# Layer 0 of a four-layer convolution stack: how the first expansion of a block, the first image's loads and the last block's residual rows are arranged

## The chip, the cores and the metric

The kernel runs on one core of one Trainium2 chip, as one launch. The metric is the device time in microseconds (us), the median of several runs. The engines are called by their short names: PE (TensorE, matmuls; PEld is its loading of stationary operands), DVE (VectorE), ACT (ScalarE), POOL (GpSimd) and SP (SyncE, which here only issues DMAs).

## The reference, cut to what matters

Input x is (4, 64, 256, 256) in float32. Four layers follow one another, each `x = x + f(groupnorm(x))`. The change touches layer 0 alone:

```python
def _L0_conv_ref(x, w_in, w_dw, fft_filter, w_out):
    p = PATCH                                             # 8
    x = jnp.einsum('bchw,oc->bohw', x, w_in)              # 64 -> 384 channels
    B, C, H, W = x.shape
    xp = x.reshape(B, C, H // p, p, W // p, p).transpose(0, 1, 2, 4, 3, 5)
    xp = jnp.fft.irfft2(jnp.fft.rfft2(xp) * fft_filter, s=(p, p))
    x = xp.transpose(0, 1, 2, 4, 3, 5).reshape(B, C, H, W)
    x = lax.conv_general_dilated(x, w_dw, window_strides=(1, 1), padding=[(1, 1), (1, 1)], feature_group_count=C)
    x1, x2 = jnp.split(x, 2, axis=1)
    x = jax.nn.gelu(x1, approximate=False) * x2
    return jnp.einsum('bchw,oc->bohw', x, w_out)          # 192 -> 64 channels
...
x = x + _L0_conv_ref(_gn(x), L0_conv_w_in, L0_conv_w_dw, L0_conv_fft_filter, L0_conv_w_out)
```

The group norm takes the mean and variance of pairs of channels over a whole image, so all of an image must have been read before any of it can be normalized.

## The kernel before, in words

**Blocks.** Layer 0 cuts each of the four images into three blocks of 11 rows of 8x8 patches (`NR = 11`), twelve blocks in all, p = 0 to 11. A block is worked through four times, kb = 0 to 3, each time for a quarter of the hidden channels. I call such a pass a quarter.

**A quarter** has two stages. The *expansion* (`expand`, L459) makes the 64-to-384 matmul with the normalized patches as the stationary operand and writes the result, patch by patch, into one SBUF tile `u`. It goes in steps (`steps_of`, L450): 11 or 12 a quarter, for eleven or twelve rows of patches. A step has two forms. With `pairs`, one stationary holds two neighbouring patches (64 x 128, L470): 16 matmuls, which the profile lists as 32 records, and four copies of 64 x 384 on ACT and four on DVE to bring the result from PSUM to `u` (L486). Without, each patch is a stationary of its own (64 x 64, L476): 32 matmuls, 64 records, and three copies on each engine (L488 to L490). The condition is on L789: the steps t = 0 to 5 of every quarter are in the first form, the rest in the second. PSUM has four tiles of two banks, and a step takes two of them, one for ACT and one for DVE.

The *convolution* joins the patchwise filter and the 3 x 3 convolution into one, by weights `wt` that are computed at the start. Per group g of four channels, `own` (L514) multiplies each patch by its own weights (L523) and `beside` (L528) adds what comes from the neighbours (L539). ACT then takes the Gelu (L546), DVE multiplies (L547), and POOL stores the tile `h` to a DRAM tile `g` (L550). The loop on L802 takes two groups at a time, g = 0, 2, ..., 10.

**The projection lags by one block.** While block p is expanded and convolved, `project` (L605) makes the 192-to-64 matmul (L627, L634) of block p - 1 in 16 units: row class r = 0 to 7 of the patch, two halves each. A unit needs two tiles read back from `g` (`load_g`, L569), and the residual rows r of the input (`load_r`, L591, rows of 128 floats, 512 bytes). DVE adds (L643 to L648), and after a second half it takes the statistics for the next layer (L654) and POOL stores the rows (L658). Each unit, when done, issues the loads of the unit two later (`unit`, L742). A block's first two units have their loads issued by the list `first`. In the first quarter the residual rows of r = 0 are ordered after step 0, the first half of `g` after the last step (L792), the second half at g = 0 (L807), and the four units stand at g = 4, 6, 8, 10. In the other three quarters the four units stand at g = 0, 2, 6, 8 (L805).

**What sets the order.** PE, DVE, ACT and SP carry out their instructions in the order in which the Python emits them; a semaphore wait holds up what is behind it on the same engine only. SP issues loads in program order and isn't held by PE's place in the program, only by free buffers and by data. POOL's order is made by the framework's scheduler.

**The start (L677 to L710).** Image 0 is read in 32 parts of 8 rows (`first_stats`, L683), and DVE takes statistics of each (`input_stats`, L313). The first ten parts read are those of block 0; they are kept in SBUF, in four tiles of the pool `p_x` and six of `p_f`, since block 0 is normalized from them. The other 22 go through three tiles of the pool `p_s`. Ahead of part 0, 10 and 20, DVE builds a table (`tables`, L334), and ACT and POOL copy it into weight tiles that POOL stores to DRAM (`weights`, L375). Then the group norm of image 0 follows (L710), whose power is taken on POOL (L217), and block 0's normalizing starts.

**The end (p = NB, L732).** After the last convolution the 16 units of the last block are left alone. The tile `u` is given up, six `g` tiles of each kind and three residual tiles take its place, and loads run three row classes ahead, on SP and ACT. Layer 1 begins by the group norm of the last image.

Of the kernel before, what the change touches and what calls it, by code (L numbers as in the profile page):

```python
# [118 lines left out]
class _Net:  # L119
# [152 lines left out]
    def _layer0(self, ctx, dst):  # L272
# [10 lines left out]
        P = PATCH  # L283
# [307 lines left out]
        def load_r(p, r):  # L591
            lo, hi, j0, rr = rows_in(p, r)
            rt = rts[p, r] = sources[p == NB - 1][2].tile([128, NR, HW2], F32, tag="r", name=f"r_{p}_{r}")[:, 0 : hi - lo]
            for s in range(2):
                nc.sync.dma_start(
                    rt[halves[s]], xr(a["x"][blocks[p][0]])[rr][:, j0 : j0 + hi - lo, s * HW2 : (s + 1) * HW2]
                )
# [79 lines left out]
        with ordered:  # L677
# [4 lines left out]

            def first_stats(k):  # L683
                if k >= NJ:
                    return
                if k < len(kept):
                    load_x(kept[k], p_x if k < 4 else p_f)
                    parts[k] = x0[kept[k]]
                    return
                t = parts[k] = p_s.tile([128, 4, W], F32, tag="x", name=f"st_{k}")  # L690
                for s in range(2):
                    nc.sync.dma_start(t[halves[s]], src_t[0, :, k, s])
# [5 lines left out]
            for k in range(len(kept) + 3):  # L698
                first_stats(k)
            copies = [nc.scalar.copy, nc.gpsimd.tensor_copy, nc.scalar.copy]  # L700
            for k in range(NJ):
                if k % 10 == 0 and k < 30:
                    tables(k // 10)
                    weights(k // 10, copies)
                input_stats(parts.pop(k), k, bst0)
                if k >= len(kept):
                    first_stats(k + 3)
# [21 lines left out]
            for p in range(NB + 1):  # L729
# [49 lines left out]
                for kb in range(4):  # L779
                    for t in range(NR + 1):  # L780
# [7 lines left out]
                        if t < len(steps):  # L788
                            expand(p, kb, steps[t], t < (NR + 1) // 2)  # L789
                        if t == 0 and kb == 0 and 0 < p:  # L790
                            load_r(p - 1, 0)
                        if t == NR:  # L792
                            if first:
                                load_half(*first.pop(0))
# [7 lines left out]
                    for g in range(0, NG, 2):  # L802
                        if g > 0:
                            load_w(p * (HID // 8) + (NG * kb + g) // 2 + 3)
                        if g in ((0, 2, 6, 8) if kb else (4, 6, 8, 10)):  # L805
                            unit()
                        if g == 0 and first:  # L807
                            load_half(*first.pop(0))
# [11 lines left out]
                        if kb == 3:  # L820
                            normalize_rows(2)
                            continue
# [734 lines left out]
```

## Time and profile before

| | us |
|---|---|
| median of 3 runs | 6439.4 |
| lowest, highest run | 6436.1, 6456.2 |
| the profiled execution, its own time | 6447.1 |
| its span, first to last instruction | 6445.2 |
| mean granted PE clock | 0.954 of full |
| norm of image 0 ready (L218, DVE) | 124.7 |
| first matmul of block 0, of block 1, of block 11 (L470) | 127.5, 395.1, 3453.2 |
| end of the last convolution of layer 0 (L539) | 3750.2 |
| end of the last projection matmul of layer 0 (L634) | 3875.9 |
| first convolution matmul of layer 1 (L940) | 3891.8 |

All times inside the execution count from the span's first instruction. In the profile's groups, a row gives line, engine, operation, output and input with the shape, then the busy time in us, the mean duration of one in ns, and the idle time ahead of them with what ended most of it. "issue" there is time in which an engine waited for nothing that the profile shows. In the table of windows, each row is a stretch, with the busy time of PE, PEld, DVE, ACT and POOL (number of instructions in brackets), the granted PE clock, the mean busy share of the 16 DMA engines and what they moved in GB/s. In the timeline, a row gives start, duration, engine, line, operation and number of instructions merged, and in square brackets the idle time ahead with what ended it.

### The profile page before, as it was taken

Reading aid. Unit: us, or ns where it says so; the run is one execution under the profiler, and the core shown is the slowest. Engines: PE = TensorE matmul, PEld = TensorE weight load, DVE = VectorE, ACT = ScalarE, POOL = GpSimd, SP = SyncE. Lnnn points to the kernel's source line nnn. Section 1 sums busy time; section 2 is a strip of 40 time slices with the busy share of each in tenths; the row PEclk is TensorE's granted clock in tenths of the full one; section 3 lists DMA queues with packets and bytes.
Section 4 is the critical chain, followed back from the end, with each engine's and each line's share of the span. In section 5 each row is a group of like instructions: output and inputs, shape, how many; then the busy total and the mean of one; then the engine's idle time right before and its main releaser. Section 6 shows DMA issues by size and latency. Waiting matters only on the chain.

```text
span 6445.2 us, 237146 instructions
## 1 busy us (share of the span) xinstructions
PE 5961.0 (92%) x106198; PEld 3303.0 (51%) x106198; DVE 4282.4 (66%) x5939; ACT 3245.7 (50%) x4575; POOL 1059.0 (16%) x1651
## 2 busy tenths in 40 slices
PE   1999999999999999999999969999899999998997
PEld 1556555555555655555565533333344444443566
DVE  5556565666566666655565638999788988885265
ACT  3444444444343535343445406777787877773211
POOL 4111111111111111111111111111122222221011
PEclk9999999999999999999999969999999999999855
DMA  7477878887888877777878699999566666678899
GB/s 198 150 216 227 224 221 231 245 228 234 224 243 235 233 217 226 224 229 223 230 217 223 191 228 239 226 230 227 145 172 172 174 173 180 173 185 278 307 362 395
DMA packets 769610, 1442.23 MB, mean 224 GB/s; under 512 B 77412, under 2 KB 463476, under 8 KB 766548
## 3 DMA queue, kind: packets, MB, share of 16 engines
q1 hardware_dynamic: 616388, 917.72, 53.7%
q0 software_dynamic: 148672, 500.14, 23.2%
q8 instruction: 839, 13.75, 0.9%
q10 hardware_dynamic: 3536, 9.20, 0.6%
q14 instruction: 175, 1.43, 0.1%
HBM read 926.71 MB, written 500.04 MB: 221 GB/s over the span
## 4 chain that ended last, share of the span: by engine, by line
PE 76%; issue 7%; DVE 7%; DMA 6%; ACT 3%; POOL 1%; SPq 0%; POOLq 0%; DVEq 0%; ACTq 0%
PE pc L539 17%; PE pc L523 11%; PE m L940 10%; PE one L1181 9%; PE div L1140 7%; PE psu L470 4%; DVE u L486 4%; PE psu L476 4%; PE po L627 4%; PE psz L1170 2%; PE po L634 2%; DMA x<-x 2%; PE psa L1368 2%; ACT u L486 1%; DMA g<-g 1%
## 5 line engine op out<-in xcount | busy, mean ns | idle before, releaser
L547 DVE TENSOR_TENSOR h<-h,pc 128x374 f32<-128x374 f32 x1152 | 576.9, 542 | 1203.4 <-ACT h L546 1203.2
L546 ACT ACTIVATE h<-pc 128x374 f32<-128x374 f32 x1152 | 495.2, 480 | 1728.7 <-PE pc L539 1727.6
L539 PE MATMUL pc<-u,w 64*16 64x374 f32 (+2 forms) x27648 | 1186.2, 479 | 12.5 <-issue 12.5
L550 POOL DMA_DIRECT2D g<-h x576 | 417.9, 726 | 2888.4 <-DVE h L547 2810.5
L523 PE MATMUL pc<-u,w 64*64 64x374 f32 x9216 | 835.8, 485 | 28.3 <-DVE u L490 21.1
L539 PEld LDWEIGHTS pc<-u,w 64*16 64x16 f32 (+2 forms) x27648 | 465.7, 92 | 698.5 <-issue 664.1
L486 DVE COPY u<-psu 64x384 f32<-64x384 f32 x1152 | 640.1, 556 | 50.6 <-PE psu L470 31.3
L470 PE MATMUL psu<-win,xn 64*128 64x96 f32 x9216 | 618.3, 277 | 36.1 <-ACT u L486 24.9
L486 ACT COPY u<-psu 64x384 f32<-64x384 f32 x1152 | 592.3, 514 | 109.8 <-PE psu L470 78.7
L470 PEld LDWEIGHTS psu<-win,xn 64*128 64x128 f32 x9216 | 582.0, 188 | 93.3 <-ACT u L486 33.6
L1126 DVE TENSOR_TENSOR q<-xn 128x2313 f32<-128x2313 f32 (+2 forms) x256 | 627.6, 2494 | 1.7 <-ACT xn L253 1.7
L1181 PE MATMUL one<-z,wp 32*32 32x512 f32 x16384 | 595.0, 597 | 21.1 <-issue 17.1
L253 ACT ACTIVATE xn<-x,nb,r 128x1024 f32<-128x1024 f32 (+3 forms) x267 | 475.3, 1802 | 204.0 <-DMA x<-x 143.1
L523 PEld LDWEIGHTS pc<-u,w 64*64 64x64 f32 x9216 | 365.9, 133 | 397.6 <-issue 158.3
L476 PE MATMUL psu<-win,xn 64*64 64x96 f32 x16384 | 468.5, 253 | 89.0 <-issue 55.3
L1127 ACT ACTIVATE q<-q 128x2313 f32<-128x2313 f32 (+2 forms) x256 | 529.0, 2087 | 31.3 <-DVE q L1126 30.2
L1181 PEld LDWEIGHTS one<-z,wp 32*32 32x32 f32 x16384 | 369.6, 103 | 227.5 <-issue 84.4
L476 PEld LDWEIGHTS psu<-win,xn 64*64 64x64 f32 x16384 | 407.3, 138 | 145.7 <-issue 83.2
L1140 PE MATMUL div<-q,ones 64*32 64x512 f32 x8192 | 469.9, 598 | 11.0 <-ACT q L1127 9.2
L1214 POOL DMA_DIRECT2D x<-r x512 | 275.7, 545 | 976.3 <-DVE r L1211 961.8
L627 PE MATMUL po<-g,wo 128*64 128x176 f32 (+1 forms) x3072 | 316.3, 348 | 64.8 <-DMA g<-g 37.9
L940 PE MATMUL m<-t,wk 64*64 64x512 f32 x3072 | 341.1, 588 | 0.0
(157 smaller groups left out, 6636.9 us busy)
## 6 DMA issues: line engine op xcount, KB each, us to landing
g<-h POOLq DMA_DIRECT2D x576, 374.0 KB, 6.9
x<-x SPq DMA_DIRECT2D x240, 640.0 KB, 6.4
w<-wt SPq DMA_DIRECT2D x288, 448.0 KB, 6.8
x<-x SPq DMA_DIRECT2D x100, 1024.0 KB, 14.1
g<-g SPq DMA_DIRECT2D x414, 187.0 KB, 7.5
g<-g SPq DMA_DIRECT2D x736, 93.5 KB, 6.9
x<-in_x_dram SPq DMA_DIRECT2D x256, 256.0 KB, 8.0
x<-o POOLq DMA_DIRECT2D x128, 512.0 KB, 8.2
```

Source lines behind the costliest of these rows:

```text
L470: nc.tensor.matmul(ps[s][:, k, at], xn[halves[s], n : n + 2].rearrange("p n r w -> p (n r w)"), win[halves[s], kb, 0 : 2 * PB], start=True ...
L476: nc.tensor.matmul(ps[s][halves[1 - odd], k, at], xn[halves[s], n + odd].rearrange("p r w -> p (r w)"), win[halves[s], kb, PB * (1 - odd) ...
L486: copy(at(h, o0 + o), v[k, c : c + PB])
L523: nc.tensor.matmul(out(C * c, C, k, h), w[halves[h], k, 2 * (G % 2) + c, 0:C], cells(h, 4 * g + 2 * k + c, 0, 0), start=True, stop=False, ...
L539: nc.tensor.matmul(out(q, m, k, h), w[halves[h], k, 2 * (G % 2) + c, c0 : c0 + m], cells(h, 4 * g + 2 * k + c, down, right), start=False, ...
L547: nc.vector.tensor_mul(h[:, k], h[:, k], ps[k][:, 1, 0:L])
L627: nc.tensor.matmul(out(k, s, x), wo1, moving(g1[:, 2 * k], 2 * half + k, s, x), start=(x == 0), stop=False, skip_group_check=True,)
L940: nc.tensor.matmul(rows2(m)[halves[j], s], w[dx][halves[s]], ts[n][halves[s], i, 2 * j : 2 * j + 2, dx : dx + W], start=(dx == 0), stop=(d ...
L1126: nc.vector.tensor_sub(d, p0, p1)
L1127: nc.scalar.activation(d, d, AF.Square)
L1140: ins = nc.tensor.matmul(ps[quarters[j], h], ones[halves[h]], q[n, g, k][halves[h], r + 2 * j : r + 2 * j + 2, o : o + W], start=(m == 0), ...
L1181: ins = nc.tensor.matmul(rows2(ps[g])[quarters[j], k], w[quarters[i]], z[quarters[i], h, 2 * j + dy : 2 * j + dy + 2, dx : dx + W], tile_p ...
```

## The change

Four edits, all in layer 0:

1. In a block's first quarter (kb = 0) all steps of the expansion take the form with two patches per stationary.
2. In that quarter the projection units stand at g = 0, 2, 6, 8, as in the others, and the loads for a block's first two units are ordered after steps 0 and 4 of the expansion (residual rows with the first).
3. At the start, the 22 parts of image 0 that are not kept are read first, through all 13 tiles (three of `p_s`, four of `p_x`, six of `p_f`), each reloaded when its statistics are done; the ten kept parts come last, into `p_x` and `p_f`.
4. In the last block, the residual rows of r = 0 to 4 are loaded in its fourth quarter, into the five tiles of `p_xn`, which held the normalized patches.

```diff
         def load_r(p, r):
             lo, hi, j0, rr = rows_in(p, r)
-            rt = rts[p, r] = sources[p == NB - 1][2].tile([128, NR, HW2], F32, tag="r", name=f"r_{p}_{r}")[:, 0 : hi - lo]
+            if p == NB - 1 and r < NR // 2:
+                rt = p_xn.tile([128, W // P, P, P], F32, tag="xn", name=f"r_{p}_{r}")
+                rt = rt.rearrange("p m r w -> p (m r w)")[:, 0 : NR * HW2].rearrange("p (i w) -> p i w", w=HW2)
+            else:
+                rt = sources[p == NB - 1][2].tile([128, NR, HW2], F32, tag="r", name=f"r_{p}_{r}")
+            rt = rts[p, r] = rt[:, 0 : hi - lo]
...
+            n_flow = NJ - len(kept)
+            places = [p_s] * 3 + [p_x] * 4 + [p_f] * 6
+
             def first_stats(k):
                 if k >= NJ:
                     return
-                if k < len(kept):
-                    load_x(kept[k], p_x if k < 4 else p_f)
-                    parts[k] = x0[kept[k]]
+                if k >= n_flow:
+                    part = kept[k - n_flow]
+                    load_x(part, p_x if k < n_flow + 4 else p_f)
+                    parts[k] = x0[part]
                     return
-                t = parts[k] = p_s.tile([128, 4, W], F32, tag="x", name=f"st_{k}")
+                t = parts[k] = places[k % 13].tile([128, 4, W], F32, tag="x", name=f"st_{k}")
                 for s in range(2):
-                    nc.sync.dma_start(t[halves[s]], src_t[0, :, k, s])
+                    nc.sync.dma_start(t[halves[s]], src_t[0, :, len(kept) + k, s])
...
-            for k in range(len(kept) + 3):
+            for k in range(13):
                 first_stats(k)
...
                 input_stats(parts.pop(k), k, bst0)
-                if k >= len(kept):
-                    first_stats(k + 3)
+                first_stats(k + 13)
...
                         if t < len(steps):
-                            expand(p, kb, steps[t], t < (NR + 1) // 2)
-                        if t == 0 and kb == 0 and 0 < p:
-                            load_r(p - 1, 0)
+                            expand(p, kb, steps[t], kb == 0 or t < (NR + 1) // 2)
+                        if t in (0, 4) and first:
+                            load_half(*first.pop(0))
                         if t == NR:
-                            if first:
-                                load_half(*first.pop(0))
                             load_w(p * (HID // 8) + NG * kb // 2 + 3)
                             load_next(kb)
...
-                        if g in ((0, 2, 6, 8) if kb else (4, 6, 8, 10)):
+                        if g in (0, 2, 6, 8):
                             unit()
-                        if g == 0 and first:
-                            load_half(*first.pop(0))
...
                         if kb == 3:
                             normalize_rows(2)
+                            if p == NB - 1 and g < 2 * (NR // 2):
+                                load_r(p, g // 2)
                             continue
```

## Prediction

> **What bounds the kernel now.** I read the page's busy shares and slices first, then the waits of TensorE (PE), its timeline in one block of layer 0, and last the two places where PE is not busy: the start and the end of layer 0.
>
> ```profile
> PE 5961.0 (92%) x106198; PEld 3303.0 (51%) x106198; DVE 4282.4 (66%) x5939; ACT 3245.7 (50%) x4575; POOL 1059.0 (16%) x1651
> PE   1999999999999999999999969999899999998997
> L486 DVE COPY u<-psu 64x384 f32<-64x384 f32 x1152 | 640.1, 556 | 50.6 <-PE psu L470 31.3
> q8 instruction: 839, 13.75, 0.9%
> ```
>
> PE is busy nearly everywhere; layer 0's two holes are slice 0 (to 161 us) and slice 23 (3706 to 3867 us). Between them what counts is PE's own stream. The next view gives one block (block 3) by quarter, that is by kb; times are us, then PE, PEld, DVE, ACT, POOL busy, clock, DMA share, GB/s.
>
> ```profile
> 1013.10:1094.80 81.70, 75.16 (x1415) 45.81 (x1410) 47.70 (x83) 30.76 (x64) 14.12 (x18) 0.96 0.80 220
> 1094.80:1170.80 76.00, 72.54 (x1413) 44.11 (x1410) 47.67 (x83) 29.97 (x63) 11.27 (x15) 0.98 0.87 245
> 1170.80:1243.90 73.10, 71.63 (x1414) 43.23 (x1408) 45.43 (x79) 30.31 (x63) 12.00 (x16) 1.00 0.76 225
> 1243.90:1316.10 72.20, 70.78 (x1416) 43.11 (x1408) 44.80 (x76) 43.07 (x74) 11.83 (x16) 1.00 0.86 248
> ```
>
> All quarters hold the same PE work, yet the first takes 9 us more. Over blocks 1 to 11 (first L470 matmul of a quarter to that of the next) the means are 81.8, 75.5, 73.9 and 73.9. PE's timeline of that first quarter says why:
>
> ```profile
> 1017.36 9.09 PE L470 MATMUL psu<-win,xn 64*128 64x96 f32 x128 [0.48 <-ACT u L486]
> 1026.38 1.91 PE L476 MATMUL psu<-win,xn 64*64 64x96 f32 x64
> ...
> 1034.74 5.86 PE L476 MATMUL psu<-win,xn 64*64 64x96 f32 x138 [2.74 <-issue]
> ...
> 1042.57 2.81 PE L523 MATMUL pc<-u,w 64*64 64x374 f32 x28 [1.24 <-DVE u L490]
> ...
> 1093.36 1.48 PE L539 MATMUL pc<-u,w 64*28 64x374 f32 x24 [1.39 <-issue]
> ```
>
> A step with two patches per stationary (L470) runs without a hole. A step with one (L476) stops for 2.74 us on nothing that the profile shows, and after the last one the convolution waits 1.24 us for evictions. In the trace's packets, queue q8 brings instructions in blocks of 16384 bytes; one starts at 1032.1, inside the hole (1031.7 to 1034.7). Two more holes, 1109.0 to 1111.9 and 1091.2 to 1093.4, hold or follow one likewise. PE runs out of instructions.
>
> The start of layer 0, by tens of us (same columns), and its end:
>
> ```profile
> 60.00:70.00 10.00, 0.00 (x0) 0.00 (x0) 3.86 (x6) 0.00 (x0) 0.69 (x2) 1.00 1.02 297
> 70.00:80.00 10.00, 0.00 (x0) 0.00 (x0) 6.55 (x17) 0.00 (x0) 0.00 (x0) 1.00 0.70 213
> 80.00:90.00 10.00, 0.00 (x0) 0.00 (x0) 7.88 (x11) 5.61 (x28) 3.25 (x13) 1.00 0.32 85
> 90.00:100.00 10.00, 0.00 (x0) 0.00 (x0) 3.86 (x6) 4.32 (x23) 10.00 (x22) 1.00 1.02 255
> ...
> 3780.00:3800.00 20.00, 12.26 (x99) 7.46 (x96) 6.10 (x7) 0.00 (x0) 1.54 (x2) 0.54 1.07 274
> ```
>
> The DMA engines are full from 10 to 70 us and again from 90; between they idle, while VectorE (DVE) builds the third table and three statistics buffers stay taken. At the end they are over-full (1.07) while PE waits.
>
> **What the Trainium skill says.** "Runtime: NRT & Kernel Launch", section "Instruction fetch mechanics", has instructions refilled in 16 KiB blocks of 256 over a DMA queue of the sequencer's own, the cost "mostly hidden". The block size agrees (839 packets, 13.75 MB); "hidden" does not (2.74 us). "TensorEngine Tiling (Array Packing)", "PSUM Bottleneck", warns that the copy out can become the bound: it does in L470 steps, whose pace of 2.22 us is four DVE copies of 556 ns. "DMA: Bandwidth & Descriptors", "Issuing engines are not separate DMA queues": all DMAs share 16 engines. The trace agrees: SP's, ACT's and POOL's packets together fill the tail.
>
> **The change part by part.**
>
> *Two patches per stationary in the first quarter.* 59 steps in blocks 1 to 11 (five each, six in blocks 1, 4, 7, 10) and 5 in block 0 go from 64 matmul records to 32, and from three copies per engine to four. Undisturbed, L476 takes 1.66 us of PE (and 1.67 of DVE), but these 59 average 2.72; an L470 step is 2.22, with no fetch hole in any quarter's six. One block of 256 instructions lasts 3.3 us of L476 (128 in 1.66 us), but 8.9 us of L470 (64 in 2.22), against holes of up to 3.1 us. So PE's part becomes 2.1 + (n-1) x 2.22 us, then the last step's own 2.1 less the 2.2 counted: 26.4 us for n = 12, 24.2 for 11, mean 25.0 over the eleven blocks, against 28.0 now.
>
> *Units at g = 0, 2, 6, 8 in the first quarter.* The unit (one projection, 2.3 us: 1056.05 to 1058.36) now stands between expansion and convolution, where it covers the last evictions (2.2 us of DVE); now that wait is 1.5 us on average. A convolution stretch with three units inside is 47.9 us in the second and third quarters; with four it is 53.9 in the first now. New first quarter: 25.0 + 2.3 + 47.9 = 75.2 against 81.8, so -6.6 x 11 = **-73 us**. On POOL the residual store moves ahead of four h stores, as it stands in the other quarters; four h buffers cover its wait for DVE, and if they did not, the next Gelu would wait.
>
> *g loads at steps 0 and 4, on SP.* They were queued at the end of the expansion, but SP isn't held by PE: it issued the first at 1008.9, waited to 1020.75 for the g store, and ended half 0 at 1023.1. With some 6.5 us to landing they are there by 1030; the unit will want them at about 1038. Cover: 8 us. Half 1 moves ahead of one weight load and one statistics load (2 us on SP; weights are ordered three pairs ahead). I count 0. The last unit's loads also leave the end of the first quarter, next to the second's expansion, which has 1.6 us more than the third's: I take half, **-9 us** (0 to -18).
>
> *Block 0.* Three instruction streams do the start. All 32 loads need 56.3 us of the 16 DMA engines (4096 packets of 220 ns), small loads 2.5, the first two weight stores 29; from 5 us on that is done by 93 us. DVE: statistics of 20 parts end near 72 us (74.6 now; that stretch is full of DMA already), the table takes 9.7 to 82, then 12 x 1.29 us, all data in, to 97.5. POOL's copies and stores for the third table follow it by 18.5 us (84.3 to 102.8 now), so to 100.5, and the norm's last step is on POOL: norm at about 103 against 124.7. That is -21.7. The turned order costs nothing, since the norm needs all 32 parts anyway. The five new steps cost +2.3: 0.55 us of copies each, less ACT time shared with normalizing, and no unit to cover the last eviction. Net **-19 us** (-10 to -24).
>
> *Residual rows of the last block.* Five of eight loads, 1408 packets of 512 bytes each, 4.17 us of all engines apiece (33.35 for eight), move before 3752 us, into 52 us that hold 29 us of DMA work. The first fell in a wait for the g store anyway (9.4 us); four count: **-16 us** (-5 to -20). PE at half clock needs 4.05 us a unit, 8.1 per row pair, against 11.3 of DMA left, so DMA still binds. In the last quarter these loads wait only for xn tiles that its expansion has read.
>
> Sum: -73 - 9 - 19 - 16 = -117 on a profiled execution of 6447.1 us (span 6445.2), 7.7 above the median of 6439.4, which gives 6330 from the one and 6322 from the other. I say **6326**.
>
> **The rivals.** (a) All parts act: 6326. (b) Fetch holes only move: PE must still get every block, and a hole may open in the next convolution instead (1.4 us there now). Then the 2.8 us of issue waits that its expansion has now, on average, come back in the convolution: -3.8 x 11 = -42, the second quarter nothing; with start -10 and tail -6, 6439 - 58 = 6381. For it: holes follow DMA traffic, which stays. Against: the third and fourth quarters, with the same convolution, show 0.2 us or less there. (c) The gain is eaten by later waits, or a part does not do what it says (residual tiles held by late xn readers): about 6435. (d) Slower: the unit at g = 0 stands first in PE's order, so if the g halves land late, PE and all convolution behind it stop, eleven times. It costs nothing up to 8 us of delay and takes the whole gain from 8 + 117/11 = 18.6 us; at 22 it gives 6439 + 3.4 x 11 = 6476. For it: the DMA share is 0.80 there. Against: the same unit stands at g = 0 in three quarters with no load wait on PE.
>
> **How the numbers follow.** (a) 0.61, own range 6298 to 6350; (b) 0.27; (c) 0.05; (d) 0.07. 6298 is every bound taken at its best; the top, 6392, takes in (b) and leaves out (c), (d). About 0.3% (19 us) is what a measurement can tell from none: faster 0.88, same 0.05, slower 0.07.
>
> **What would show it.** Right: first quarters near 75 us; no issue hole in their expansions; no DVE wait at their first L523; first normalize near 103 us; DMA share near 1 from 70 to 90 us; last projection near 16 us after layer 0's last convolution less than now. Wrong: PE waits on g at the first L627; holes in the first convolution; the third table's stores later than 103.

## The result, and the profile after

| | before | after |
|---|---|---|
| median, us | 6438.6 (4 runs) | 6344.8 (4 runs, 6344.1 to 6345.0) |
| ratio | | 0.9848 [0.9831, 0.9866] |
| the profiled execution, own time and span | 6447.1, 6445.2 | 6345.0, 6343.0 |
| mean granted PE clock | 0.954 | 0.960 |
| norm of image 0 ready (L218) | 124.7 | 99.9 |
| first matmul of block 0, of block 1 | 127.5, 395.1 | 107.0, 376.1 |
| end of the last convolution of layer 0 | 3750.2 | 3670.4 |
| end of the last projection of layer 0 | 3875.9 | 3776.8 |

94 us faster by the medians, 98 by the ratio and 102 by the two profiled executions, of which before's was 8 us slower than its median; forecast was 6326, 113 below. Line numbers up to L550 are those of before; the unit's matmuls are now L632 and L639 (L627, L634 before).

The page's first part and slices, the groups of copies, and the instruction queue, of the kernel after:

```profile
PE 5965.4 (94%) x104150; PEld 3328.8 (52%) x104150; DVE 4315.4 (68%) x6003; ACT 3274.7 (52%) x4639; POOL 1054.2 (17%) x1651
...
PE   3999999999999999999999969999899999999987
...
q8 instruction: 823, 13.48, 0.9%
...
L486 DVE COPY u<-psu 64x384 f32<-64x384 f32 x1408 | 782.3, 556 | 60.4 <-PE psu L470 36.4
```

PE is busy for as long as before (5965 us against 5961) in a span that is 102 us shorter, so what went is, in sum, idle time. The first slice has two tenths more. The copies of L486 are 256 more, at the same 556 ns each. Edit 1 takes 2048 matmuls out of the program (64 steps by 32), and as many weight loads; these 4096 instructions are the 16 blocks of 256 by which q8's packets fall.

Block 3 by quarters, windows of the kernel after (columns as before):

```profile
979.00:1055.40 76.40, 74.86 (x1256) 46.63 (x1248) 50.32 (x88) 32.85 (x68) 13.38 (x17) 1.00 0.94 260
1055.40:1129.80 74.40, 72.22 (x1418) 42.95 (x1410) 47.58 (x83) 30.28 (x63) 12.02 (x17) 1.00 0.80 230
1129.80:1202.10 72.30, 71.11 (x1410) 43.00 (x1408) 45.45 (x79) 30.27 (x63) 11.91 (x16) 1.00 0.77 220
1202.10:1275.20 73.10, 70.88 (x1416) 44.10 (x1408) 44.79 (x76) 42.92 (x74) 11.78 (x16) 1.00 0.87 248
```

The first quarter is 76.4 long, not 81.7, and its PE hardly idles (1.5 us, 6.5 before). PE's timeline of it:

```profile
979.01 3.81 PE L470 MATMUL psu<-win,xn 64*128 64x96 f32 x64
983.31 20.57 PE L470 MATMUL psu<-win,xn 64*128 64x96 f32 x288 [0.48 <-ACT u L486]
1003.81 1.62 PE L632 MATMUL po<-g,wo 128*64 128x176 f32 x16
1005.36 0.93 PE L639 MATMUL po<-g,wo 64*64 64x176 f32 x16
1006.12 2.77 PE L523 MATMUL pc<-u,w 64*64 64x374 f32 x32
1008.81 4.07 PE L539 MATMUL pc<-u,w 64*16 64x374 f32 x96
...
1041.43 2.81 PE L523 MATMUL pc<-u,w 64*64 64x374 f32 x27 [0.57 <-issue]
```

The holes of 2.74 us (issue) and 1.24 us (evictions) are gone: nine steps of L470 run through in 20.57 us, then the unit stands where PE used to wait for DVE, and the convolution starts without a wait. The nine steps also give a pace, 20.57 / 9 = 2.29 us a step, that I had taken as 2.22. One hole of 0.57 us is left, in a convolution.

The clock column of these windows shows a cost of a hole that its own length doesn't hold. In block 3 of before, the granted clock is 0.5 for 6.83 us, from inside the hole of 2.74 us on:

```profile
1033.65:1040.48 6.83, 5.74 (x141) 5.74 (x142) 3.34 (x6) 3.08 (x6) 0.00 (x0) 0.50 0.33 93
```

In blocks 1 to 11 before has 14 such stretches, of 3.41 or 6.83 us, 54.6 us in all. Each begins in an idle time of PE of 1.75 us or more, or within 1.3 us of its end; 14 of 19 such idle times are followed by one, and none of 212 shorter ones is. After has 5, 17.1 us in all. A record of L476 takes 43 ns of PE in them and 28 elsewhere. By these paces the half clock cost about 21 us before and 6 after, which is an estimate: some 14 of the 102 us are work that no longer runs at half clock.

Waits of PE from the first matmul of block 0 to the end of layer 0's last convolution (total, times, longest):

```profile
PE psu L470 <- ACT u L486: 26.7, 51, 1.3
PE psu L476 <- issue: 18.4, 28, 3.1
...
PE pc L539 <- issue: 4.5, 4, 1.9
...
PE pc L523 <- DVE u L490: 3.4, 4, 1.2
```

For the same stretch, before had 55.3 us for L476 at issue, 12.5 for L539 at issue and 21.1 for L523 at the evictions of L490. The start, by tens of us, and a stretch of the end, windows of after:

```profile
60.00:70.00 10.00, 0.00 (x0) 0.00 (x0) 9.33 (x20) 0.00 (x0) 1.56 (x3) 1.00 1.03 361
70.00:80.00 10.00, 0.00 (x0) 0.00 (x0) 8.86 (x14) 8.39 (x42) 6.01 (x16) 1.00 0.97 295
80.00:90.00 10.00, 0.00 (x0) 0.00 (x0) 5.05 (x8) 1.55 (x9) 9.71 (x22) 1.00 1.01 298
90.00:100.00 10.00, 1.17 (x4) 1.00 (x4) 5.22 (x10) 0.00 (x0) 0.87 (x2) 1.00 1.02 273
3700.00:3720.00 20.00, 11.33 (x112) 7.21 (x106) 9.31 (x12) 0.00 (x0) 3.08 (x4) 0.80 1.01 283
```

From 70 to 90 us the DMA share was 0.70 and 0.32 and is now 0.97 and 1.01: the transfers no longer pause. At the end the engines are as full as before; there is only less to move. But behind the norm there is a new wait, in the waits of POOL from 60 to 110 us:

```profile
POOL u L767 <- DMA w<-wt: 4.4, 1, 4.4
```

POOL clears the borders of `u` in the place of a table (L767), and that place is free only when the last weight stores have landed. The line above names a load (`w<-wt`); the chain of the same execution has a store, to 103.98:

```profile
89.52 14.46 DMA wt<-T
```

The norm is ready at 99.9, the clear ends at 105.8, and block 0's first matmul follows at 107.0.

Profile to profile the sum closes. Start, to the first matmul: 127.5 to 107.0, -20.4. Block 0: +2.1 in its first quarter, -0.6 in the others. Blocks 1 to 11, means of a quarter times 11: first 81.80 to 76.01, -64; second 75.47 to 74.36, -12; third 73.91 to 74.22, +3; fourth 73.93 to 75.03, +12 (block 11's, which no L470 step follows, counted like the ten others). End, from the last convolution to the last projection: 125.7 to 106.4, -19. Layers 1 to 3: -3. In all -102.

### The profile page after: what moved, and what is told of

Same layout as the page of the kernel before. It is cut to its first block, busy times and chain, and to the rows that moved or that the text cites. A ratio compares the mean times of both kernels' runs of the same rounds, so it can differ in the third digit from the quotient of the medians.

```text
span 6343.0 us, 233229 instructions
## 1 busy us (share of the span) xinstructions
PE 5965.4 (94%) x104150; PEld 3328.8 (52%) x104150; DVE 4315.4 (68%) x6003; ACT 3274.7 (52%) x4639; POOL 1054.2 (17%) x1651
## 4 chain that ended last, share of the span: by engine, by line
PE 83%; DVE 6%; DMA 6%; ACT 3%; issue 2%; POOL 0%; SPq 0%; ACTq 0%; POOLq 0%; DVEq 0%
PE pc L539 18%; PE pc L523 12%; PE m L946 10%; PE one L1187 9%; PE psu L470 8%; PE div L1146 7%; PE po L632 4%; DVE u L486 4%; PE psu L476 3%; PE psz L1176 2%; PE po L639 2%; ACT u L486 2%; PE psy L1521 2%; PE psa L1374 2%; DMA x<-x 2%
## 5 line engine op out<-in xcount | busy, mean ns | idle before, releaser
L539 PE MATMUL pc<-u,w 64*16 64x374 f32 (+2 forms) x27648 | 1178.0, 479 | 4.7 <-issue 4.5
L550 POOL DMA_DIRECT2D g<-h x576 | 415.5, 721 | 2834.5 <-DVE h L547 2724.2
L523 PE MATMUL pc<-u,w 64*64 64x374 f32 x9216 | 832.0, 484 | 10.1 <-DVE u L490 3.4
L486 DVE COPY u<-psu 64x384 f32<-64x384 f32 x1408 | 782.3, 556 | 60.4 <-PE psu L470 36.4
L539 PEld LDWEIGHTS pc<-u,w 64*16 64x16 f32 (+2 forms) x27648 | 465.5, 92 | 682.0 <-issue 645.4
L470 PE MATMUL psu<-win,xn 64*128 64x96 f32 x11264 | 759.9, 277 | 47.7 <-ACT u L486 26.7
L486 ACT COPY u<-psu 64x384 f32<-64x384 f32 x1408 | 722.8, 513 | 128.2 <-PE psu L470 100.8
L470 PEld LDWEIGHTS psu<-win,xn 64*128 64x128 f32 x11264 | 714.4, 188 | 114.3 <-ACT u L486 36.2
L523 PEld LDWEIGHTS pc<-u,w 64*64 64x64 f32 x9216 | 363.9, 132 | 383.5 <-issue 159.1
L476 PE MATMUL psu<-win,xn 64*64 64x96 f32 x12288 | 345.6, 250 | 39.9 <-issue 18.4
L632 PE MATMUL po<-g,wo 128*64 128x176 f32 (+1 forms) x3072 | 315.2, 348 | 45.0 <-DMA g<-g 36.9
L476 PEld LDWEIGHTS psu<-win,xn 64*64 64x64 f32 x12288 | 299.8, 135 | 82.3 <-issue 34.5
## 6 DMA issues: line engine op xcount, KB each, us to landing
g<-h POOLq DMA_DIRECT2D x576, 374.0 KB, 6.7
```

The lines of the kernel that those rows point to most:

```text
L470: nc.tensor.matmul(ps[s][:, k, at], xn[halves[s], n : n + 2].rearrange("p n r w -> p (n r w)"), win[halves[s], kb, 0 : 2 * PB], start=True ...
L476: nc.tensor.matmul(ps[s][halves[1 - odd], k, at], xn[halves[s], n + odd].rearrange("p r w -> p (r w)"), win[halves[s], kb, PB * (1 - odd) ...
L486: copy(at(h, o0 + o), v[k, c : c + PB])
L523: nc.tensor.matmul(out(C * c, C, k, h), w[halves[h], k, 2 * (G % 2) + c, 0:C], cells(h, 4 * g + 2 * k + c, 0, 0), start=True, stop=False, ...
L539: nc.tensor.matmul(out(q, m, k, h), w[halves[h], k, 2 * (G % 2) + c, c0 : c0 + m], cells(h, 4 * g + 2 * k + c, down, right), start=False, ...
L632: nc.tensor.matmul(out(k, s, x), wo1, moving(g1[:, 2 * k], 2 * half + k, s, x), start=(x == 0), stop=False, skip_group_check=True,)
```

## The experiments

The theory is the prediction's: PE runs out of instructions in L476 steps of the first quarter, since these use them up faster than they are fetched while DMA traffic is heavy; L470 steps don't, and so edit 1 closes the holes. The first rival is that holes only move, and that what brought the gain was something else (the unit as a cover, or the start). For the start, the theory is that transfers had idled; for the end, that the volume of DMA counts.

**Each edit alone on the kernel before** (before's median beside them: 6445.3). The edits are those of the diff of the change, shortened here.

```diff
-                if k < len(kept):
-                    load_x(kept[k], p_x if k < 4 else p_f)
+                if k >= n_flow:
+                    part = kept[k - n_flow]
+                    load_x(part, p_x if k < n_flow + 4 else p_f)
...
-            for k in range(len(kept) + 3):
+            for k in range(13):
                 first_stats(k)
```

> The kernel before with only the turned order of image 0's loads (edit 3). Theory (the four edits act apart and add up): the norm of image 0 comes near 100 us, the first L470 matmul near 107 instead of 127.5, and the whole is 20 us shorter, since the rest of the program is the same. Rival (the earlier start is given back later, for instance because the weight stores then collide with block 0): under 12 us shorter.

Edit 3 alone: 6424.3, ratio 0.9972 [0.9961, 0.9982], -18 us by the ratio. First matmul at 108.2 against 127.5, and POOL waits 4.6 us for the same clear. The theory held: this part is worth what the profile of after shows, and it comes with its own new wait.

```diff
+                            if p == NB - 1 and g < 2 * (NR // 2):
+                                load_r(p, g // 2)
```

> The kernel before with only the early residual rows of the last block (edit 4). Theory (the end of layer 0 is bound by its DMA volume): the stretch from the last convolution matmul to the last projection matmul falls from 125.7 to about 106 us, the whole by 19 us. Rival (the chain of waits binds, not the volume): under 8 us, with the DMA share of that stretch falling below 0.9 instead.

Edit 4 alone: 6420.4, 0.9961 [0.9946, 0.9975], -25, of which the trace shows 22. From the last convolution to the last projection 104.1 us against 125.7. In these 104.1 us all DMA packets together take 100.1 us of the 16 engines: still bound by volume, as the theory had it.

```diff
-                            expand(p, kb, steps[t], t < (NR + 1) // 2)
+                            expand(p, kb, steps[t], kb == 0 or t < (NR + 1) // 2)
```

> The kernel before with only the two-patch form in all steps of the first quarter (edit 1); the units stay at g = 4, 6, 8, 10. Theory A (the fetch of instructions is most of what the first quarter loses): 3 to 4 us less in each of eleven first quarters, from the 2.8 us of issue waits in the expansion and the 1.1 us in the convolution, so 35 to 45 us in all. Theory B (the place of the units and their loads is most of it): the expansion loses 1.6 us or less, the wait for the last evictions stays at 2 us, 15 us in all.

Edit 1 alone: 6447.2, 0.9997 [0.9988, 1.0006]. Nothing, and here the forecast of the theory failed; the rival's was nearer. The trace splits it. The issue wait in first expansions does fall, from 2.80 us to 0.35 on average. But the first quarter is only 1.8 us shorter (81.8 to 80.0). PE's timeline in block 3 of this kernel:

```profile
1018.07 20.57 PE L470 MATMUL psu<-win,xn 64*128 64x96 f32 x288 [0.48 <-ACT u L486]
1038.57 1.16 PE L523 MATMUL pc<-u,w 64*64 64x374 f32 x4
1040.68 2.81 PE L523 MATMUL pc<-u,w 64*64 64x374 f32 x28 [0.96 <-ACT u L486]
```

Without a unit ahead of the convolution the last eviction stays on PE's path (the convolution waits 1.69 us for other engines in a first quarter, 1.78 before), and the convolution keeps 0.58 us of its issue holes. Block 0 pays 2.2 us. 1.8 x 11 - 2.2 is 18 us, which the other quarters take back: they were 0.3, 0.5 and 0.6 us longer each, which adds to 15, and is within what unchanged quarters differ from one profiled execution to the next (first quarters with none of edits 1 and 2 took 81.8, 81.2 and 81.0 in three kernels, so the 1.8 itself may be 1). That this last part is chance I can't show.

```diff
-                        if t == 0 and kb == 0 and 0 < p:
-                            load_r(p - 1, 0)
+                        if t in (0, 4) and first:
+                            load_half(*first.pop(0))
...
-                        if g in ((0, 2, 6, 8) if kb else (4, 6, 8, 10)):
+                        if g in (0, 2, 6, 8):
                             unit()
```

> The kernel before with only the units at g = 0, 2, 6, 8 and the g loads after steps 0 and 4 (edit 2). Theory A (fetch is most of it): the wait of the first convolution matmul goes (1.5 us in each of eleven first quarters), the issue waits stay, 15 to 25 us in all. Theory B (the place of the units and their loads is most of it): the convolution loses 4 us and the second quarter's expansion 1.4 us, 50 us or more in all.

Edit 2 alone: 6412.0, 0.9945 [0.9933, 0.9957], -35, between the two forecasts. What theory B named came: the waits of the first convolution for other engines go (1.78 to 0.08 us a quarter), what follows the expansion in a first quarter falls from 54.5 to 51.1 us, and the second quarter gains 1.7. But the first expansion grows from 27.3 to 29.0 us. Its timeline in block 3:

```profile
1022.84 1.87 PE L476 MATMUL psu<-win,xn 64*64 64x96 f32 x77 [1.10 <-issue]
1025.00 1.49 PE L476 MATMUL psu<-win,xn 64*64 64x96 f32 x49 [0.29 <-ACT u L490]
1031.05 0.92 PE L476 MATMUL psu<-win,xn 64*64 64x96 f32 x15 [4.56 <-issue]
1031.89 2.58 PE L627 MATMUL po<-g,wo 128*64 128x176 f32 x16
```

Between the two holes lie 77 + 49 = 126 matmuls with as many weight loads, 252 instructions: one block of 256. The packet that ends the second hole starts only at 1028.4, behind six us in which the DMA engines are full. With the loads that edit 2 brings into the expansion the holes grow: 4.70 us of issue waits a first expansion, 2.80 before. In blocks 1 to 8, where the next image is read at the same time for its statistics, it is 4.5 to 6.6 (1.5 to 4.8 before); in blocks 9 to 11, which have no next image, 1.5 to 3.2 (0.7 to 2.2 before).

```diff
+                            expand(p, kb, steps[t], kb == 0 or t < (NR + 1) // 2)
+                        if t in (0, 4) and first:
...
+                        if g in (0, 2, 6, 8):
```

> The kernel before with edits 1 and 2 together. Alone they gave nothing and 33 us, the start 18, the early residual rows 25, and all four 98. Theory (the two work on each other: moving the loads into the first expansion doubles the fetch holes of its L476 steps, 2.8 to 4.7 us, and the two-patch form removes them all): 50 to 60 us faster than the kernel before, with expansions of 25.8 us and issue waits below 0.5 us in the first quarter. Rival (the start or the end gains more beside the others, and the two only add up): 30 to 38 us.

Edits 1 and 2 together, without 3 and 4 (its before 6443.7): 6384.0, 0.9909 [0.9893, 0.9926], -59, as the theory had it. First quarter 75.95, issue waits of its expansion 0.30. Alone they gave 2 (edit 1) and 35 (edit 2); together they give 59. Edit 2 needs edit 1 for its own loads not to starve PE, and edit 1 needs edit 2 to get the last eviction off the path. All parts: 18 + 25 + 59 = 102 by the ratios, from two sets of runs, against 98 by the ratio of the whole change; the intervals are wider than the difference.

**The form of the steps, on the kernel after** (before's median beside the next four: 6444.8).

```diff
-                            expand(p, kb, steps[t], kb == 0 or t < (NR + 1) // 2)
+                            expand(p, kb, steps[t], t % 2 == 0)
```

> The changed kernel with the two forms of a step in turn (two patches per stationary where t is even) in all four quarters. Fetch theory (PE runs out of instructions because L476 steps stand in a row: 128 records in 1.66 us, a block of 256 in 3.3 us; in turn with L470 steps a block lasts over 5 us, longer than the longest hole of 3.1): issue waits in the expansions below 0.4 us a quarter everywhere, expansions of 23 us in all quarters (25.8, 23.9, 23.6 and 25.2 now), 40 to 65 us faster than the changed kernel. Rival (an L476 step loses its time by itself, through its evictions or its own waits, wherever it stands): the holes stay with the L476 steps, and the time is within 15 us of the changed kernel's or above.

L470 and L476 steps alternate in every quarter: 6445.7, 0.9999 [0.9991, 1.0008], which is 100 us slower than after. The fetch theory forecast that mixing would spread the demand and close the holes. It failed, for three reasons. Issue waits grew, in the second quarter the least (1.80, 0.57, 1.39, 2.75 us; after has 0.35, 0.48, 0.29, 1.27). With them came 95.6 us of half clock in blocks 1 to 11 (17.1 in after), which by the paces of the records cost some 30 us more than in after, an estimate. And a third thing was at work that I had left out; PE's timeline in block 0's second quarter, where there is no issue hole:

```profile
180.81 2.20 PE L470 MATMUL psu<-win,xn 64*128 64x96 f32 x32 [0.79 <-ACT u L486]
182.94 1.55 PE L476 MATMUL psu<-win,xn 64*64 64x96 f32 x64
185.39 2.12 PE L470 MATMUL psu<-win,xn 64*128 64x96 f32 x32 [0.90 <-ACT u L486]
187.44 1.55 PE L476 MATMUL psu<-win,xn 64*64 64x96 f32 x64
189.69 2.26 PE L470 MATMUL psu<-win,xn 64*128 64x96 f32 x32 [0.70 <-ACT u L486]
```

Two steps take 185.39 - 180.81 = 4.6 and 189.69 - 185.39 = 4.3 us, of which PE works 3.7. PSUM holds only two steps, so with the forms in turn all L470 steps use the same one of the two places. Each keeps it for its matmuls (about 2.1 us) and then for its four copies (2.22), and only then can the next L470 step begin: 2.1 + 2.2 is 4.3, a pair of steps. In two runs of one form, six and then five, each run goes at the pace of its own slower engine and the lag is paid once: that quarter's expansion takes 22.7 us in after. Seven copies for a pair of steps would be 3.9 us. This lockstep is my reading of the timeline; no run with more or less PSUM tests it.

```diff
-                            expand(p, kb, steps[t], kb == 0 or t < (NR + 1) // 2)
+                            expand(p, kb, steps[t], t % 2 == 0 if kb == 0 else t < (NR + 1) // 2)
```

> The changed kernel with the two forms in turn in the first quarter only (six of eleven or twelve steps with two patches), the other quarters as they are. Fetch theory: no holes come back, and the eviction-bound pace falls from 2.29 to about 1.98 us a step, 2.5 us a first quarter, 25 to 30 us faster than the changed kernel. Rival (the g loads of the first quarter starve any L476 step there): issue waits of 2 us or more in its expansions, as with the units moved alone (4.7 us), and no gain or up to 15 us slower.

The same, in first quarters alone: 6344.1, 0.9844 [0.9832, 0.9857], not to be told from after; the fetch theory had forecast 25 to 30 us less. First quarter 76.5 us, issue waits 1.19 and eviction waits 2.74 (after: 0.35 and 0.72), in an expansion of the same 25.9 us. That all steps of a first quarter are L470 is thus not needed: what the waits take, the shorter L476 steps give back.

```diff
-                            expand(p, kb, steps[t], kb == 0 or t < (NR + 1) // 2)
+                            expand(p, kb, steps[t], True)
```

> The changed kernel with two patches per stationary in all steps of all quarters. Theory (an L470 step costs four DVE copies, 2.29 us, and never starves; an L476 step costs 1.7 plus its holes): the expansions of the second to fourth quarters become 25.8 us like the first, issue waits below 0.4 us, which is 1.9, 2.2 and 0.6 us more than now, so 40 to 60 us slower than the changed kernel. Rival (holes cost more than the traces show): equal or faster.

All steps of all quarters in the L470 form: 6418.3, 0.9956 [0.9943, 0.9968], 73 us slower than after. The quarters are 77.6, 76.2, 76.0 and 75.9: issue waits fall to 0.4 to 0.6 everywhere, but a steady L470 expansion is 25.7 to 26.1 us, against 23.6 to 25.2 for the mixed ones of after. So the L470 form is worth its longer evictions only where holes cost more than these, in the first quarter. This is what the theory had, but 73 lies above its 40 to 60. The first quarter, whose code is that of after, is 1.6 us longer too, of which 0.8 are issue waits behind its expansion; the cause of that stays open.

```diff
-            for j in range(3):
-                load_w(j)
...
                                 for part in first_parts[len(kept) :]:
                                     load_x(part)
+                                for j in range(3):
+                                    load_w(j)
```

> The changed kernel with the first three weight loads of block 0 ordered on SP after the load of its eleventh input part, and not ahead of the norm. Theory (in the changed kernel the clearing of u waits 4.4 us, until 104.3 us, for the last weight stores to leave the memory that u takes over, and these share the DMA engines with the three weight loads, 1.4 MB): the clearing starts by 101 us, and the first L470 matmul near 103.5 instead of 107.0, 3 to 4 us in all. Rival (the stores' own length sets it): first matmul at 106 or later, no gain.

The first weight loads, which read back what the stores wrote, are moved behind block 0's first step, to test the new wait at L767. Result 6345.9, 0.9844 [0.9831, 0.9857]: no gain that can be measured. In the trace:

```profile
102.90 1.47 POOL L765 MEMSET u<- 128x1632 f32 x1 [1.58 <-DMA wt<-T]
```

With the loads out of the way, the wait that is left (1.6 us) is named after the stores. The clear starts at 102.9 (104.3 in after), the first matmul comes at 105.6 (107.0), and block 1 starts at 374.0 (376.1). The wait is real, about half of what I forecast is to be had in the trace, and the total doesn't show it.

**Traffic and place** (before's median: 6443.7).

```diff
-                            expand(p, kb, steps[t], kb == 0 or t < (NR + 1) // 2)
+                            expand(p, kb, steps[t], kb == 0 or t < (NR + 1) // 2 or (p == 0 and kb == 3))
+                        if t == 0 and p == 0 and kb > 0:
+                            for k in range(12):
+                                nc.sync.dma_start(junk[k], a["x"][B - 1, :, 8 * k : 8 * k + 8, :])
```

> The changed kernel with 12 copies of 0.5 MB from DRAM to DRAM, which nothing reads, ordered at the beginning of the second, third and fourth quarters of block 0, and two patches per stationary in all steps of the fourth. Block 0 has little DMA traffic, and its expansions have issue waits of 0.2 to 0.8 us now. Theory (what delays the fetch of instructions is other traffic on the DMA engines, and L476 steps use a block up before the next is there): 2 us or more of issue waits in the expansions of the second and third quarters, below 0.7 us in the fourth. Rival (holes come from the instruction stream or the block's place, not from traffic): 0.2 to 0.8 us in all three. Block 0 may be longer as a whole; the total says nothing.

In block 0, where after has no issue holes to speak of, 12 copies of 0.5 MB from DRAM to DRAM are added at the start of the second, third and fourth quarter, and the fourth quarter's steps all take the L470 form. The copies are used by nothing. It was run once, for its trace. Block 0's second to fourth quarters in this kernel, and then in after:

```profile
179.90:252.20 72.30, 64.89 (x1286) 39.10 (x1282) 38.45 (x71) 30.31 (x63) 8.70 (x13) 0.95 0.73 220
252.20:325.10 72.90, 66.03 (x1286) 39.72 (x1282) 36.05 (x67) 30.30 (x63) 8.71 (x13) 0.95 0.65 202
325.10:393.30 68.20, 65.74 (x1122) 39.76 (x1120) 36.51 (x68) 45.63 (x79) 8.68 (x12) 1.00 0.97 284
```

```profile
179.90:245.00 65.10, 62.90 (x1283) 37.02 (x1280) 38.45 (x71) 30.27 (x63) 8.67 (x12) 1.00 0.48 148
245.00:310.60 65.60, 62.91 (x1288) 37.00 (x1280) 36.06 (x67) 30.27 (x63) 8.71 (x12) 1.00 0.43 136
310.60:376.10 65.50, 62.79 (x1290) 36.75 (x1282) 33.66 (x63) 42.68 (x74) 8.72 (x13) 1.00 0.70 200
```

The second and third quarters grow by 7 us each: 5 us of new issue waits, and 6.83 us of half clock behind them (the 0.95 of the clock column). The fourth grows by 2.7, though its DMA share is the highest (0.97), and the form itself accounts for that: without copies, in the kernel with all steps in the L470 form, the same quarter took 68.2 too. Waits of PE in this kernel's expansions, third quarter:

```profile
PE psu L476 <- issue: 5.4, 3, 3.0
```

and fourth quarter:

```profile
PE psu L470 <- ACT u L486: 1.1, 3, 0.5
...
PE psu L470 <- issue: 0.4, 1, 0.4
```

5.4 us of holes with L476 steps under the copies, 0.4 with L470 steps under the same copies, and 0.3 in after's third quarter with L476 steps and no copies. Both halves of the theory are seen in this one execution: traffic makes the holes, and the L470 form is all but immune. The copies load the DRAM as well as the DMA engines; which of the two delays the fetch is not shown.

```diff
-                            expand(p, kb, steps[t], kb == 0 or t < (NR + 1) // 2)
+                            expand(p, kb, steps[t], t >= len(steps) - (NR + 1) // 2 if kb == 0 else t < (NR + 1) // 2)
```

> The changed kernel with the first quarter's forms the other way round: one patch per stationary in its first five or six steps, two in the last six. Steps in turn gave no gain because PE and the evictions then go in lockstep, 2.2 us a step; in two runs they cost 5.3 x 1.67 + 6 x 2.29 = 22.6 us and a start of 1, against 25.8 now. Theory (holes come when the g loads and input loads run, from 8 us into the expansion on, and the L476 steps now lie before that): issue waits below 1 us, 20 to 27 us faster than the changed kernel. Rival (the fetch is late there too, behind the last unit's loads and the convolution): issue waits of 2 us or more, gain below 10 us.

In first quarters, L476 steps first and six L470 steps last: 6339.8, 0.984 [0.9826, 0.9853], not to be told from after (0.9848 [0.9831, 0.9866]), where I had forecast 20 to 27 us less; the rival's forecast is the one that came. Block 0's first quarter gains 4.1 us (68.7), but in blocks 1 to 11 the first expansion has 3.09 us of issue waits again and the quarter takes 76.6.

```diff
-                            expand(p, kb, steps[t], kb == 0 or t < (NR + 1) // 2)
+                            expand(p, kb, steps[t], t >= len(steps) - (NR + 1) // 2)
```

> The changed kernel with the forms the other way round in all four quarters. Theory (as in the run with the first quarter alone; in the others the L476 steps also come ahead of the new loads): the other expansions, 23.9, 23.6 and 25.2 us now, come to 23 to 23.5, 20 us more than the reversed first quarter alone gains, so 35 to 50 us faster than the changed kernel. Rival (the loads of the last unit, at g = 8, are in flight there): issue waits of 1.5 us or more in the second to fourth quarters, slower than the reversed first quarter alone.

That order in all quarters: 6538.5, 1.0148 [1.0134, 1.0162], some 194 us slower than after. The quarters are 77.4, 77.8, 79.3 and 81.6, and the expansions have 2.9, 3.9, 4.5 and 5.6 us of issue waits. Half clock adds to it: 222 us in blocks 1 to 11 (17.1 in after), which by the paces of the records is some 70 us of the 194, an estimate. Block 0 tells where the holes come from. Its second to fourth expansions have 2.0, 3.6 and 2.5 us of issue waits, with the same loads as in after, where they have 0.4 at most. PE's timeline in its third quarter:

```profile
244.07 0.54 PE L539 MATMUL pc<-u,w 64*4 64x374 f32 x8
244.54 4.70 PE L476 MATMUL psu<-win,xn 64*64 64x96 f32 x179
249.65 1.87 PE L476 MATMUL psu<-win,xn 64*64 64x96 f32 x77 [0.40 <-issue]
251.83 1.47 PE L476 MATMUL psu<-win,xn 64*64 64x96 f32 x49 [0.31 <-ACT u L490]
256.49 0.63 PE L476 MATMUL psu<-win,xn 64*64 64x96 f32 x15 [3.19 <-issue]
257.05 8.75 PE L470 MATMUL psu<-win,xn 64*128 64x96 f32 x96
```

The same spacing of one block (77 + 49 matmuls), and an end of the holes with the first L470 step. What differs from after is which steps meet the loads. These come at the head of a quarter, and for the same 7 us the DMA engines are full. Here these are L476 steps (first row); in after they are L470 steps (second row), and its L476 steps run when the engines are idle (third row):

```profile
246.00:253.00 7.00, 6.24 (x245) 5.46 (x240) 6.21 (x12) 5.79 (x12) 0.73 (x1) 1.00 1.01 291
246.00:253.00 7.00, 6.52 (x107) 6.21 (x104) 6.37 (x13) 5.63 (x11) 0.72 (x1) 1.00 0.97 305
258.30:268.00 9.70, 8.84 (x320) 7.68 (x321) 9.16 (x17) 8.20 (x16) 0.00 (x0) 1.00 0.02 3
```

So the order of the forms counts because of traffic, at the moment and not on average. Before, after, `units_only`, `alt_all`, `loads_in_block0`, `reversed_first` and `reversed_all` have 175 issue holes of over 1 us in layer 0's expansions and convolutions; in 167 of them the DMA share is 0.8 or more in the 4 us ahead of the packet that ends the hole. The rates fit. By the timeline of after above, a group of the convolution uses 128 matmuls and 128 weight loads in 6.7 us (1006.1 to 1012.8), 38 instructions a us; an L470 step uses 64 in 2.29, 28 a us; an L476 step 128 in 1.66, 77 a us. When the engines are idle, as in the L476 steps of before's third quarters, the blocks of 256 come 3.2 to 4.5 us apart, 57 to 80 a us; under the copies in `loads_in_block0` two late ones came 6.6 us apart (270.9 and 277.5), 39 a us. That is too few for L476 steps, enough for L470 steps, and just enough for a convolution.

The same holds between the quarters of the kernel before: in the first 2 us of their L476 steps the mean DMA share was 1.06, 0.67, 0.02 and 0.52 in first to fourth quarters of blocks 1 to 11, and the issue waits of the expansions were 2.80, 1.68, 0.35 and 0.66 us. Whether a slower stage also leaves the fetch a store to live on, as a convolution might not, is not shown.

No kernel of these was measurably better than after.

## Why the prediction was right, and where its sizes were off

The direction and the mechanism held; the time was 19 us above the forecast, in its own range. By the prediction's steps:

- **Two patches per stationary: holes go.** Right: issue waits of first expansions fell from 2.80 to 0.35 us, in the convolution from 1.1 to 0.1, so that holes did not move there (rival b). The holes begin a little later than the prediction has them (1032.0, 1109.4 and 1092.0 by the trace), which changes nothing in the reading, and L470 steps weren't quite without holes: 1.5 us in three in before, 0.9 at most. What a hole costs beyond its length, the half clock behind it, the prediction had inside its measured 28.0 us without naming it. "Runtime: NRT & Kernel Launch", section "Instruction fetch mechanics", of the Trainium skill has the refill in blocks of 256 as a sequential stream; the spacing of 252 counted instructions between holes agrees. Its "mostly hidden" holds for L470 steps; in the L476 steps of after 18.4 us remain.
- **The pace of an L470 step, 2.22 us.** Mis-sized: 2.29 (nine steps in 20.57). Four copies of 556 ns are busy time; there are gaps between them, since 24 copies take 13.74 us, not 13.34. The trace of before had this already: the prediction's own line has four steps in 9.09 us, 2.27 each. Expansions measured 24.9 us (11 steps) and 27.2 (12), forecast 24.2 and 26.4; mean 25.8, not 25.0. With 0.3 more for the unit and 0.3 less for the convolution (47.6), the first quarter is 76.0, not 75.2: 0.8 x 11 = 9 us of the 15 by which the profiled time misses the sum (-102 for -117).
- **The gain split by edit.** The working gave holes to edit 1 and evictions to edit 2, as if each stood by itself. Together the terms were right (-5.8 a quarter for -6.6), but alone edit 1 gave nothing measurable, and edit 2 paid half of what it gained in the first quarter (3.4 us) back in a longer expansion (1.7). It was right for the change as a whole and would have been wrong for a half of it.
- **g loads at steps 0 and 4, counted as 0.** No wait of PE on g at g = 0 in first quarters: the loads are hidden, and rival (d) had no ground. What I left out is that they delay the fetch: without edit 1 they cost 4.70 - 2.80 = 1.9 us of issue waits a first expansion.
- **Second quarter, -9.** -12. As argued there, the last unit's loads have left its expansion: the mean DMA share of its first 13.7 us fell from 1.03 to 0.73.
- **Fourth quarter, not forecast.** +1.1 us each, +12. Five kernels that leave this quarter as it is (the four edits alone, and 1 with 2) have 74.1 to 74.8, where before had 73.9 and after 75.0, so part of it is a low draw of the one profiled execution of before. After's fourth expansions have also the most issue waits (1.27 us; 0.66 to 1.20 in the others), and 1.2 us of half clock each, where before's have none. Whether the change causes some of it stays open.
- **Start, -19.** -20.4 to the first matmul and +2.1 in block 0's first quarter (forecast +2.3), -18 in sum. Within it two errors cancel: the third table ended at 71.5, not at 82, since the parts ahead of it arrived sooner, and the norm was ready at 99.9, not at 103; then the clear of `u` took the place of the norm as the last thing to wait for (4.4 us), a wait that I hadn't looked for. "DMA: Bandwidth & Descriptors", section "Issuing engines are not separate DMA queues", named in the prediction, fits here again: weight stores issued by 90.3 share the engines with the x loads, and the last lands some 14 us later (from 85 to 108 us POOL's queue had 51% of the engines' time, that of the loads 48%).
- **End, -16 (-5 to -20).** -19.3 in the trace. I let four of five loads count, and all five left the stretch: packets of 512 bytes fell from 11136 to 4096, that is by five times 1408, and their time from 33.3 to 11.2 us of all engines. All packets together then take 103 us of the stretch's 106.4.

The misses of the sum (15 us) are mostly two that point the same way: 9 of the pace and 12 of the fourth quarter. The third quarters, not forecast either, add 3; the second quarters, the end and layers 1 to 3 take off 3 each.

## What to carry to other kernels

When PE idles on "issue" in a stream of small matmuls, count its instructions a microsecond there, and look at the DMA share in the few microseconds ahead of the hole, not at its average: a stage that uses more than the fetch brings under full DMA engines should run where they are idle, and a form with fewer instructions should stand where the loads come. Count the granted clock behind a hole with the hole. A shorter stage is worth nothing while the wait behind it stays; ask of two edits whether each needs the other, and cost them as a pair. And where there is place for two steps only, alternating long and short ones gives all long ones the same place; here that was slower than two runs of one form.

## What the runs showed of the hardware that was not expected

- PE's instructions come as packets on the DMA engines (queue q8, 0.9% of their time), and other traffic delays them: 6 MB of plain copies raised the holes of an expansion from 0.3 to 5.4 us. In before PE went on 1.5 us (median of 35 holes; 1.3 to 1.6) after the packet of an instruction block had ended.
- A granted clock of 0.5, for 3.41 us or a multiple of it, followed 14 of the 19 idle times of PE of 1.75 us or more in blocks 1 to 11 of before, and none of 212 shorter ones.
- In layer 0 of before, from 100 to 3700 us, a 512-byte packet took 44 ns of a DMA engine on average, one of 2992 bytes 165, one of 4096 bytes 218: rows of 512 bytes cost about 1.6 times as much for the same bytes. Five residual loads of such rows took 22 of the 33 us of all engines that 512-byte packets had in the end stretch.
- Alternating forms through two steps of PSUM took 4.3 to 4.6 us for a pair in which PE works 3.7 us and DVE's seven copies 3.9.
